# A two-layer cross-attention kernel: the context of later batches loaded in 32x32 blocks and turned by VectorE, and a new order for the work that prepares the next batch

## The chip, the cores and the metric

The kernel runs on one core of a Trainium2 chip. The metric is the device time of one execution in microseconds; lower is better. Three runs are given as their median, and one further execution was recorded by the profiler.

## The reference

Four sequences of 1024 rows, `x` of width 512 and a context of width 384, go through two cross-attention layers in float32. Cut to what matters:

```python
def layer0(x, context):                      # 16 heads of 64
    h = layernorm(x) * gamma + beta
    Q, K, V = h @ Wq, context @ Wk, context @ Wv
    attn = softmax(Q @ K.T, axis=-1) * 64 ** -0.5          # per head
    return x + (attn @ V) @ Wo + bo

def layer1(x, context):                      # 16 heads of 32
    xn = x * rsqrt(mean(x * x) + 1e-5) * norm_w
    q, k, v = xn @ wq, *split(context @ wkv)
    q, k = l2_normalised(rotary(q)), l2_normalised(rotary(k))
    attn = softmax(q @ k.T * sqrt(32), axis=-1)
    return x + (attn @ v) @ wout

out = layer1(layer0(x, ctx), ctx)            # the same context in both
```

## The kernel before

The batches are worked one after another. For each of them layer 0 goes through eight pairs of heads, each in eight steps of 128 query rows; then layer 1 goes through two halves of eight heads, each in 32 steps. TensorE multiplies with the feature dimension on the partitions, so it needs both the context and the normalised `x` turned: `cT` (tag `ctxT`, one buffer, 128 x 3 x 1024) and `hT` (two halves of 128 x 4 x 512).

The order in which instructions are issued is written out by the kernel itself; the scheduler does not move them. Every engine works through its own queue in that order. A class `Units` holds a queue of small pieces of other work, each with an estimated cost. Each attention step calls `fill(us)`, which issues pieces until the allowance of the step is spent. A piece with cost 0.0 is issued as soon as its turn comes. In layer 1 the allowance is the total cost left divided by the steps left, so the pieces are spread evenly.

A step of layer 1 (`Attention1.step`) issues, in this order: eight score matmuls (L576) for 128 keys times two and 256 queries; two exponentials on ScalarE (L586) into one of two halves of the tile `e`; the product of the step before (`finish`, `product`: L615), which after every fourth step is followed by the row sums, eight matmuls with `ones` (L626) over the tile `both`; then the pieces of other work; and last the additions on VectorE that collect the exponentials (two of L592 a step, and L596 in the two middle steps of four). A reciprocal and a product (L633, L634) divide after every fourth step. The row sums of one group of four are thus issued in the first step of the next group, and need the additions of all four steps.

The second half of layer 1 is where the next batch is prepared (`prepare_units`, `order`). Its pieces are:

- the context: four row tiles `c` of 128 x 384 a half, loaded on SP (L181), turned by TensorE against an identity into PSUM (L190) and copied to `cT` by ScalarE (L136);
- `x`: four tiles `xr` of 128 x 512 a half (L272), statistics on VectorE (L214, L215), a reciprocal square root on GpSimd (L168), the application on VectorE (L231), a turn on TensorE (L246) and a scaled copy on ScalarE (L248);
- the projections of the first two pairs of heads of the next batch: keys `k` and values `v` from `cT`, queries `q` from `hT` (helper `matmul`, L164);
- the additions of this batch's own first two output groups to `x` (`adds`, split in six parts by `some(i)`): two projection pieces for each of eight row tiles, and one VectorE addition (L294).

The tiles `c` and `xr` share the tag `row` with four buffers, so each group of four must be turned before the next can be loaded. The weights of a pair (tag `wpair`, two buffers) are loaded by `begin` of the pair before (L306). All of these loads are issued by SP, in order, and a load whose buffer is not free stops SP until it is.

The cost of preparing is paid in three of the four batches, since the first is prepared before anything else and has its own order.

Of the kernel before, what the change touches and what calls it, by code (L numbers as in the profile page):

```python
# [31 lines left out]
F32 = mybir.dt.float32  # L32
# [4 lines left out]
P = 128  # L37
S = 1024
NT = S // P
DQ = 512  # L40
NQ = DQ // P
DC = 384
NC_ = DC // P
# [65 lines left out]
def xattn_kernel(ctx: ExitStack, tc: tile.TileContext, a: dict, out: bass.AP):  # L109
    nc = tc.nc  # L110
    x, c = a["x"], a["ctx_768"]
# [3 lines left out]
    sb = ctx.enter_context(tc.tile_pool(name="sb", bufs=2))  # L115
# [10 lines left out]
    def bank(name):  # L126

        while True:
            which["n"] = which["n"] + 1 if which["n"] < 3 else which["from"]
            if which["n"] != which["kept"]:  # L130
                break
            which["kept"] = None
        return ps_f.tile([P, 512], F32, tag=f"f{which['n']}", name=name)

    def evac(dst, src):
        nc.scalar.copy(dst, src)  # L136
# [22 lines left out]
    def matmul(o, lhsT, rhs, start, stop):  # L159

        w = P // which["cols"]
        for j in range(which["cols"]):
            rr = slice(j * w, (j + 1) * w)
            nc.tensor.matmul(o[rr], lhsT[:, rr], rhs, start=start, stop=stop)  # L164
# [5 lines left out]

    def context_units(b, ct):

        raws = {}

        def load(h):
            for t in range(4 * h, 4 * h + 4):
                if b == 0 and h:
                    raws[t] = sb.tile([P, S], F32, tag="vals", bufs=4, name=f"c_{b}_{t}")[:, :DC]
                else:
                    raws[t] = sb.tile([P, DC], F32, tag="row", bufs=4, name=f"c_{b}_{t}")  # L180
                nc.sync.dma_start(raws[t], c[b, t * P : (t + 1) * P, :])  # L181

        def turn_over(h, k):
            if k == 0:
                if h == 0:
                    both = sb.tile([P, NC_, S], F32, tag="ctxT", bufs=1, name=f"cT_{b}")
                    ct.extend([both[:, :, :512], both[:, :, 512:]])
            pp = bank(f"ptc_{b}_{h}_{k}")
            for t in range(4):
                nc.tensor.transpose(pp[:, t * P : (t + 1) * P], raws[4 * h + t][:, k * P : (k + 1) * P], ident)  # L190
            evac(ct[h][:, k, :], pp)

        return [
            {
                "load": [(0.0, lambda h=h: load(h))],
                "turn": [(0.45, lambda h=h, k=k: turn_over(h, k)) for k in range(NC_)],
            }
            for h in range(2)
        ]
# [109 lines left out]
    def pair_units(b, p, w, hT, ct, res):  # L309

        n = f"{b}_{p}"

        def project(what, src, w0, nk, h, k, st={}):
            if what == "kT" and h == 0 and k == 0:
                qk = sb.tile([P, 2, S], F32, tag="qk", bufs=3, name=f"qk0_{n}")
                res["kT"], res["qT"] = qk[:, 0], qk[:, 1]
            if k == 0:
                st["pp"] = bank(f"p{what}0_{n}_{h}")
            matmul(st["pp"], w()[:, w0 + k, :], src[h][:, k, :], k == 0, k == nk - 1)
            if k < nk - 1:  # L320
                return
            if what == "qT":
                evac(res[what][:, h * 512 : (h + 1) * 512], st["pp"])
            else:
                quarters = res[what].rearrange("p (g c i) -> p c g i", g=4, i=32)
                evac(quarters[:, 4 * h : 4 * h + 4], st["pp"].rearrange("p (c g i) -> p c g i", g=4, i=32))

        def values(h, t, st={}):
            if h == 0 and t == 0:
                res["v"] = sb.tile([P, NT, P], F32, tag="v", bufs=3, name=f"v0_{n}")  # L330
            if t == 0:
                st["pp"] = bank(f"pv0_{n}_{h}")
            for k in range(NC_):
                matmul(
                    st["pp"][:, t * P : (t + 1) * P],
                    ct[h][:, k, t * P : (t + 1) * P],
                    w()[:, NQ + NC_ + k, :],
                    k == 0,
                    k == NC_ - 1,
                )  # L340
            if t == 3:
                evac(res["v"][:, 4 * h : 4 * h + 4, :].rearrange("p t f -> p (t f)"), st["pp"])

        return {
            "k": [(0.86, lambda h=h, k=k: project("kT", ct, NQ, NC_, h, k)) for h in range(2) for k in range(NC_)],
            "q": [(0.86, lambda h=h, k=k: project("qT", hT, 0, NQ, h, k)) for h in range(2) for k in range(NQ)],
            "v": [(0.66, lambda h=h, t=t: values(h, t)) for h in range(2) for t in range(4)],
        }
# [296 lines left out]
    def flat(lists):  # L645
        return [u for lst in lists for u in lst]

    def prepare_units(b):

        st = {"ct": [], "hT": [], "pairs": [{} for _ in range(NPAIR)]}  # L650
        w = {}

        def load():
            w[0] = pair_load(b, 0)

        def project(p):
            def begin():
                if p + 1 < NPAIR:
                    w[p + 1] = pair_load(b, p + 1)

            begin = {"begin": [(0.0, begin)]}
            return begin | pair_units(b, p, lambda: w[p], st["hT"], st["ct"], st["pairs"][p])

        st["project"] = lambda p: flat(project(p).values())
        cts = context_units(b, st["ct"])
        norms = norm_units(b, 0, st["hT"], load_rows(b))

        def order(other):

            pairs = [project(p) for p in range(2)]  # L670
            n = len(other)

            def some(i):
                return flat(other[n * i // 6 : n * (i + 1) // 6])

            if b == 0:
                loads = [cts[0]["load"], cts[1]["load"], norms[0]["load"], [(0.0, columns_load)]]
                loads += [norms[1]["load"], pairs[0]["begin"], [(0.0, constants_load)]]
                first = cts[0]["turn"] + norms[0]["stats"] + pairs[0]["k"][:NC_] + norms[0]["apply"]
                first += cts[1]["turn"] + pairs[0]["k"][NC_:] + norms[1]["stats"]  # L680
                first += norms[0]["turn"] + pairs[0]["q"][:NQ] + norms[1]["apply"]
                rest = pairs[0]["v"] + norms[1]["turn"] + pairs[0]["q"][NQ:]
                later = flat([pairs[1][c] for c in ("begin", "k", "q", "v")])
                return [(0.0, load)] + flat(loads) + first, rest, later
            return flat(
                [
                    [(0.0, load)] + cts[0]["load"] + some(0) + cts[0]["turn"],
                    cts[1]["load"] + some(1) + cts[1]["turn"],
                    norms[0]["load"] + some(2) + norms[0]["stats"] + pairs[0]["begin"] + pairs[0]["k"],
                    norms[0]["apply"] + some(3) + norms[0]["turn"],  # L690
                    norms[1]["load"] + pairs[0]["v"] + norms[1]["stats"] + some(4),
                    norms[1]["apply"] + some(5) + norms[1]["turn"] + pairs[0]["q"],
                    pairs[1]["begin"] + pairs[1]["k"] + pairs[1]["q"],
                ]
            ), pairs[1]["v"]

        return st, order

# [2 lines left out]
    first, rest, later = order([])  # L701
# [13 lines left out]
    for b in range(B):  # L715
        ct, hT, pairs = st["ct"], st["hT"], st["pairs"]
# [6 lines left out]
        for p in range(NPAIR):  # L723
# [10 lines left out]
            elif p % 2 == 0:  # L734
                i = p // 2 - 1
# [3 lines left out]
                    lambda n, i=i: wo[i][:, n % 2, :],  # L739
# [6 lines left out]
            if p == 6:  # L746
# [5 lines left out]
                k = rotated_chains(lambda kq=kq: kq["k"], ct, NC_, lambda k, wk=wk: wk[:, k, :], f"k1_{b}_0", RowScratch())  # L752
                other = [(0.0, lambda: begin("k"))] + k[0][0] + flat(outs[:2]) + k[1][0] + k[0][2] + flat(outs[2:4])
            if p == NPAIR - 1:
# [5 lines left out]
                norms = norm_units(b, 1, xnT, lambda h: xt[4 * h : 4 * h + 4])  # L760
                v = []
# [10 lines left out]
            n = 7 * (p == 0)  # L772
# [10 lines left out]
            for i in range(NT):  # L783
# [8 lines left out]
                n = NT * (NPAIR - p) - i  # L792
# [16 lines left out]
        kT, qT = kq["k"], kq["q"]  # L809
        kT1, qT1 = qk_tile(f"k1_{b}_1"), sb.tile([P, 2, S], F32, tag="raw", bufs=1, name=f"q1_{b}_1")  # L810
        q = rotated_chains(lambda kq=kq: kq["q"], xnT, NQ, lambda k, wq=wq: wq[0][:, k, :], f"q1_{b}_0", tmp)
# [19 lines left out]
        for half in range(2):  # L831
            n = 0
            if half == 0:
                vs = value_chains(att1.v1, wv1, ct, f"pv1_{b}_1")
                first = [q[1], (norms[1]["stats"], [], []), vs[0], (norms[1]["apply"], [], k1[1][2]), k1[2]]
# [11 lines left out]
            else:  # L847
# [4 lines left out]
                if b + 1 < B:  # L852
                    st, order = prepare_units(b + 1)
                    first, later = order(adds)
# [24 lines left out]
            kT, qT, v = kT1, qT1, att1.v1  # L879
# [48 lines left out]
```

## Time and profile before

| | |
|---|---|
| median of three runs | 2922.01 us (2919.55 to 2923.83) |
| the profiled execution | 2913.88 us, span 2912.1 us |
| granted TensorE clock, mean | 0.999 |
| TensorE busy | 2852.3 us (98%) |
| VectorE busy | 2186.5 us (75%) |
| ScalarE busy | 1434.4 us (49%) |
| GpSimd busy | 935.1 us (32%) |
| turns of the context on TensorE (L190) | 96 of 128x128, 24 for each batch |
| copies of turned context on ScalarE | 24 of 128x512, mean 608 ns |
| turns of the attention weights on VectorE (L400) | 512 of 128x1024, mean 1229 ns |
| context loads | 32 of 192 KB, 3.8 us to landing (median) |

The busy shares are of the whole span. A busy TensorE is not TensorE at its peak, because matmuls overlap and their ends are modelled. A timeline row gives the start, the time from the first start to the last end of the merged instructions, the engine, and in brackets the idle time before it and what ended it. A row of the stretches gives, for each engine in turn (TensorE, its weight loads, VectorE, ScalarE, GpSimd), its busy time and number of instructions, then the granted clock, the mean busy share of the 16 DMA engines and the rate in GB/s. A row of waits gives the total, the number and the longest.

### The profile page before, as it was taken

The page shows a single profiled execution, that of the slowest core. Times are in us where ns is not written, and L with a number is a line of the kernel's source. Part 1 is how long each engine was busy: PE and PEld are TensorE (multiplying, and loading weights), DVE is VectorE, ACT ScalarE, POOL GpSimd, SP SyncE. Part 2 cuts the span into 40 slices and gives each one's busy share as a digit, 9 for nine tenths or more (in the row PEclk, how much of TensorE's full clock was granted, in tenths as well). Part 3 has the DMA queues.
Part 4 walks back from the last instruction along what each step waited for, and adds up shares of the span by engine and source line. Part 5 has one row for each costly group of instructions (what it writes and reads, how often), then busy time and mean ns, then how long its engine had stood idle before and what let it go on. Part 6 is the DMA issues. An engine that isn't in the chain of part 4 may idle for free.

```text
span 2912.1 us, 66608 instructions
## 1 busy us (share of the span) xinstructions
PE 2852.3 (98%) x27336; PEld 1433.1 (49%) x27336; DVE 2186.5 (75%) x2952; ACT 1434.4 (49%) x2265; POOL 935.1 (32%) x776
## 2 busy tenths in 40 slices
PE   8999999999999999999999999999999999999998
PEld 4444455555444444555544445455554445445544
DVE  5677785878777778587777777858777777785877
ACT  4444444666534444466644444446664444444664
POOL 2343353420134335432024433534102343353300
PEclk9999999999999999999999999999999999999999
DMA  5887775010398777401039887730104988772000
GB/s 142 191 185 184 167 171 127 22 36 25 79 198 191 181 173 174 117 22 36 26 88 213 193 184 166 177 91 22 36 25 113 210 192 187 163 174 74 2 2 31
DMA packets 177553, 348.88 MB, mean 120 GB/s; under 512 B 37600, under 2 KB 93152, under 8 KB 177248
## 3 DMA queue, kind: packets, MB, share of 16 engines
q1 hardware_dynamic: 175920, 343.96, 50.1%
q8 instruction: 216, 3.54, 0.5%
q14 instruction: 89, 0.73, 0.1%
q10 hardware_dynamic: 1328, 0.66, 0.1%
HBM read 67.64 MB, written 8.39 MB: 26 GB/s over the span
## 4 chain that ended last, share of the span: by engine, by line
PE 84%; DVE 8%; SPq 3%; DMA 2%; issue 1%; ACT 1%; POOL 1%; DVEq 0%; ACTq 0%
PE s L366 16%; PE av L427 14%; PE po L164 11%; PE s L576 8%; PE pv L164 7%; PE pqT L164 7%; PE av L615 7%; PE pkT L164 5%; PE q_p L164 3%; SPq L411 2%; PE av L626 2%; PE k_p L164 2%; DVE both L592 2%; DMA eT<-e 1%; DVE both L596 1%
## 5 line engine op out<-in xcount | busy, mean ns | idle before, releaser
L391 DVE TENSOR_REDUCE m<-s 128x1 f32<-128x1024 f32 x512 | 603.0, 1219 | 374.9 <-PE s L366 374.4
L586 ACT ACTIVATE e<-s 128x1024 f32<-128x1024 f32 x512 | 496.7, 1022 | 312.4 <-PE s L576 303.9
L397 POOL TENSOR_SCALAR raw<-raw,li 128x1024 f32<-128x1024 f32 x256 | 286.1, 1118 | 724.2 <-DVE li L396 715.7
L366 PE MATMUL s<-qk 64*128 64x512 f32 x2048 | 515.5, 615 | 2.9 <-ACT e L392 2.2
L392 ACT ACTIVATE e<-s,m 128x1024 f32<-128x1024 f32 x256 | 282.9, 1110 | 466.5 <-DVE m L391 217.4
L392 ACT ACTIVATE raw<-s,m 128x1024 f32<-128x1024 f32 x256 | 285.3, 1115 | 454.8 <-DVE m L391 454.8
L427 PE MATMUL av<-eT,v 128*64 128x256 f32 x4096 | 470.1, 382 | 8.2 <-DMA eT<-e 6.9
L397 POOL TENSOR_SCALAR e<-e,li 128x1024 f32<-128x1024 f32 x256 | 286.0, 1118 | 474.3 <-DVE li L396 247.7
L592 DVE TENSOR_TENSOR both<-e 128x512 f32<-128x512 f32 x512 | 341.9, 700 | 114.2 <-ACT e L586 86.9
L427 PEld LDWEIGHTS av<-eT,v 128*64 128x64 f32 x4096 | 286.2, 137 | 227.2 <-issue 88.6
L366 PEld LDWEIGHTS s<-qk 64*128 64x128 f32 x2048 | 183.7, 186 | 281.5 <-issue 165.4
L576 PE MATMUL s<-q,k 32*128 32x256 f32 x4096 | 306.0, 401 | 5.8 <-ACT q L503 2.7
L400 DVE STREAM_TRANSPOSE e<-raw 128x1024 f32<-128x1024 f32 x256 | 309.9, 1228 | 0.4 <-DMA eT<-e 0.4
L400 DVE STREAM_TRANSPOSE e<-e 128x1024 f32<-128x1024 f32 x256 | 310.0, 1229 | 0.2
L576 PEld LDWEIGHTS s<-q,k 32*128 32x128 f32 x4096 | 192.1, 184 | 152.7 <-ACT e L586 71.4
L164 PE MATMUL pqT<-hT,w 128*64 128x512 f32 (+1 forms) x1216 | 240.6, 595 | 2.4 <-ACT hT L248 2.4
L164 PE MATMUL po<-wo,vals 128*64 128x512 f32 x1024 | 234.6, 596 | 0.0
L294 DVE TENSOR_TENSOR x<-x,po 128x512 f32<-128x512 f32 x200 | 131.2, 678 | 89.4 <-PE po L164 88.8
L164 PEld LDWEIGHTS pv<-w,cT 128*64 128x64 f32 (+1 forms) x3360 | 170.4, 132 | 41.6 <-issue 34.8
L164 PE MATMUL pv<-w,cT 128*64 128x128 f32 (+1 forms) x3360 | 184.3, 274 | 0.7 <-ACT hT L248 0.7
L164 PE MATMUL pkT<-cT,w 128*64 128x512 f32 (+1 forms) x912 | 183.7, 598 | 0.0
L596 DVE TENSOR_TENSOR both<-both 128x1024 f32<-128x1024 f32 x128 | 159.7, 1248 | 4.4
(81 smaller groups left out, 2784.6 us busy)
## 6 DMA issues: line engine op xcount, KB each, us to landing
eT<-e SPq DMA_DIRECT2D x2048, 128.0 KB, 2.4
xr<-in_x_dram SPq DMA_DIRECT2D x32, 256.0 KB, 3.8
wo<-in_Wo_dram SPq DMA_DIRECT2D x16, 512.0 KB, 4.7
x<-in_x_dram SPq DMA_DIRECT2D x32, 256.0 KB, 3.8
out_dram<-x SPq DMA_DIRECT2D x32, 256.0 KB, 2.6
w<-in_Wq_dram SPq DMA_DIRECT2D x31, 256.0 KB, 3.1
c<-in_ctx_dram SPq DMA_DIRECT2D x32, 192.0 KB, 3.8
wkv<-in_wkv_dram SPq DMA_DIRECT2D x16, 384.0 KB, 3.3
```

The costliest lines, as they stand in the source:

```text
L164: nc.tensor.matmul(o[rr], lhsT[:, rr], rhs, start=start, stop=stop)
L366: nc.tensor.matmul(sc[j][:, kb * 512 : (kb + 1) * 512], pr["qT"][r[j], i * P : (i + 1) * P], pr["kT"][r[j], kb * 512 : (kb + 1) * 512], st ...
L391: nc.vector.tensor_reduce(m[:, j : j + 1], sc[j], AX.X, ALU.max, negate=True)
L392: nc.scalar.activation(e[j], sc[j].rearrange("p (g s) -> p g s", g=4), AF.Exp, bias=m[:, j : j + 1], accum_out=l[:, j : j + 1])
L397: nc.gpsimd.tensor_scalar(e[j], e[j], li[:, j : j + 1], HD0**-0.5, ALU.mult, ALU.mult)
L400: self.turn = [lambda j=j: nc.vector.transpose(self.e[:, :, i % BQ * 2 + j, :], e[j]) for j in range(2)]
L427: nc.tensor.matmul(av[r[j], :W].rearrange("p (t a i) -> p t a i", t=BQ, a=4), pr["v"][:, k, r[j]], eT[:, j, :, :, k * 32 : (k + 1) * 32], ...
L576: nc.tensor.matmul(sc[j // 2][:, j % 2, c, :], kT[rr, g, k * P : (k + 1) * P], qT[rr, g, qb * WQ : (qb + 1) * WQ], start=True, stop=True,)
L586: nc.scalar.activation(e, sc[u], AF.Exp, scale=float(np.sqrt(np.float32(HD1))))
L592: nc.vector.tensor_add(self.both[:, kk, 2 * u : 2 * u + 2, :], es[u][:, :, 0, :], es[u][:, :, 1, :])
L596: nc.vector.tensor_add(self.both[:, 0], self.both[:, 0], self.both[:, kk])
L615: nc.tensor.matmul(self.av[rr, 0, :], v[g][:, 2 * kk + c, rr], es[j // 2][:, j % 2, c, :], start=first and c == 0, stop=end and c == 1,)
```

## The change

For the later three batches the context is no longer loaded as rows. Twelve DMAs write it straight into `cT`, each taking 32 features of all 1024 rows to 32 partitions, in pieces of 32 floats, so that every 32x32 block stands at its place but is not turned. Six VectorE instructions then turn the blocks in place, each over 128 x 512. The turns on TensorE and the copies on ScalarE are gone for these batches. The first batch keeps the old way.

The order of the pieces in the second half of layer 1 is also new. `x` is loaded, normalised and turned first, then the queries of both pairs are projected; the turn of the context's blocks comes after that, and the keys and values of pair 0 and the keys of pair 1 stand at the end. A small condition in `project` lets the queries of a pair come before its keys.

```diff
     def context_units(b, ct):
         raws = {}
+        def load_blocks():
+            both = sb.tile([P, NC_, S], F32, tag="ctxT", bufs=1, name=f"cT_{b}")
+            ct.extend([both[:, :, :512], both[:, :, 512:]])
+            rows = c[b].rearrange("(n i) m -> i n m", i=32)
+            for k in range(NC_):
+                for g in range(4):
+                    f = k * P + g * 32
+                    dst = both[g * 32 : (g + 1) * 32, k, :].rearrange("p (n m) -> p n m", m=32)
+                    nc.sync.dma_start(dst, rows[:, :, f : f + 32])
+
+        def turn_blocks(k):
+            for h in range(2):
+                nc.vector.transpose(ct[h][:, k, :], ct[h][:, k, :])
+
+        if b > 0:
+            return {
+                "load": [(0.0, load_blocks)],
+                "turn": [(0.0, lambda k=k: turn_blocks(k)) for k in range(NC_)],
+            }
...
         def project(what, src, w0, nk, h, k, st={}):
-            if what == "kT" and h == 0 and k == 0:
+            if not "kT" in res:
                 qk = sb.tile([P, 2, S], F32, tag="qk", bufs=3, name=f"qk0_{n}")
...
-            return flat(
+            first = flat(
                 [
-                    [(0.0, load)] + cts[0]["load"] + some(0) + cts[0]["turn"],
-                    cts[1]["load"] + some(1) + cts[1]["turn"],
-                    norms[0]["load"] + some(2) + norms[0]["stats"] + pairs[0]["begin"] + pairs[0]["k"],
-                    norms[0]["apply"] + some(3) + norms[0]["turn"],
-                    norms[1]["load"] + pairs[0]["v"] + norms[1]["stats"] + some(4),
-                    norms[1]["apply"] + some(5) + norms[1]["turn"] + pairs[0]["q"],
-                    pairs[1]["begin"] + pairs[1]["k"] + pairs[1]["q"],
+                    [(0.0, load)] + norms[0]["load"] + cts["load"] + some(0) + norms[0]["stats"] + some(1),
+                    norms[0]["apply"] + some(2) + norms[0]["turn"],
+                    norms[1]["load"] + some(3) + norms[1]["stats"] + pairs[0]["begin"] + pairs[0]["q"][:NQ] + some(4),
+                    norms[1]["apply"] + some(5) + norms[1]["turn"] + pairs[0]["q"][NQ:],
+                    pairs[1]["q"] + cts["turn"] + pairs[0]["k"] + pairs[0]["v"] + pairs[1]["begin"] + pairs[1]["k"],
                 ]
-            ), pairs[1]["v"]
+            )
+            return first, pairs[1]["v"]
```

## The prediction

> **What bounds the kernel now.** First the page's busy shares, then a table of stretches: the second halves of layer 1, in which the next batch is prepared, run from about 628 to 755 us, 1351 to 1478 and 2069 to 2196; the change lies in these three alone.
>
> ```profile
> PE 2852.3 (98%) x27336; PEld 1433.1 (49%) x27336; DVE 2186.5 (75%) x2952; ACT 1434.4 (49%) x2265; POOL 935.1 (32%) x776
> ...
> 632.00:745.00 113.00, 112.73 (x1596) 58.35 (x1592) 86.47 (x121) 72.74 (x87) 3.07 (x4) 1.00 0.13 39
> ```
>
> TensorE is busy 112.7 of 113 us there. Work taken off it is time gained, unless a wait replaces it; and any wait of TensorE is lost for good. VectorE is busy 86.5 of 113, so it has slack on the mean, not in every step. The list of waits shows where its slack ends:
>
> ```profile
> PE av L626 <- DVE both L592: 15.4, 9, 2.2
> ```
>
> Line 626, the row sums, comes every fourth step and needs VectorE's additions (L592, L596) of the step before; 15.4 us in nine places is TensorE's largest wait of its own. The timeline of TensorE prices what is removed:
>
> ```profile
> 634.37 1.53 PE L190 MATMUL ptc<-ident,c 128*128 128x128 f32 x12
> 635.94 1.07 PE L164 MATMUL po<-wo,o 128*32 128x512 f32 x8
> ...
> 642.17 1.53 PE L190 MATMUL ptc<-ident,c 128*128 128x128 f32 x12
> 643.63 1.15 PE L576 MATMUL s<-q,k 32*128 32x256 f32 x16
> ```
>
> Twelve transposes take 635.94 - 634.37 = 1.57 us, and the second twelve 643.63 - 642.17 = 1.46. The timeline of VectorE gives the prices that the change shuffles (from one start to the next):
>
> ```profile
> 632.43 0.69 DVE L294 TENSOR_TENSOR x<-x,po 128x512 f32<-128x512 f32 x1 [4.47 <-PE po L164]
> 633.03 1.29 DVE L592 TENSOR_TENSOR both<-e 128x512 f32<-128x512 f32 x2
> 634.24 1.75 DVE L633 RECIPROCAL rest<-rest 128x256 f32<-128x256 f32 x1
> 636.02 0.42 DVE L634 TENSOR_TENSOR o<-rest 128x256 f32<-128x256 f32 x1
> 636.36 1.29 DVE L592 TENSOR_TENSOR both<-e 128x512 f32<-128x512 f32 x2
> ...
> 655.42 0.69 DVE L214 BATCH_NORM_STATS2 st<-xr 128x6 f32<-128x512 f32 x1
> ...
> 658.62 1.26 DVE L592 TENSOR_TENSOR both<-e 128x512 f32<-128x512 f32 x2
> 659.92 1.22 DVE L596 TENSOR_TENSOR both<-both 128x1024 f32<-128x1024 f32 x1
> 661.06 2.57 DVE L592 TENSOR_TENSOR both<-e 128x512 f32<-128x512 f32 x4
> ...
> 665.82 1.91 DVE L231 TENSOR_SCALAR xr<-xr,mv,rs 128x512 f32<-128x512 f32 x4
> 667.65 1.28 DVE L592 TENSOR_TENSOR both<-e 128x512 f32<-128x512 f32 x2
> ```
>
> An x addition is 0.60, a pair of L592 1.21 (1.31 ahead of L596), L596 1.14, reciprocal and product 1.78 + 0.34, four statistics 3.20, four applications 1.83. Before the change, statistics come in step 6 and their application two steps later, after line 626 has passed.
>
> **What the Trainium skill says.** "VectorE: DVE Perf Modes", The three transpose paths: VectorE turns 32x32 blocks only, which is why the load must place the blocks; the trace has such an instruction (L400, 1229 ns for 128x1024). "TensorE: Matmul & The Clock Gate", Part 4: a TensorE transpose lands in PSUM and needs a copy after it; the trace agrees (24 copies cT<-ptc, 609 ns at the median), and its 273 ns per record overlaps, so I use 0.13. "DMA: Bandwidth & Descriptors", Specifications: below 512 B a transfer misses the full rate, by a read-modify-write; no 128 B load is in this trace. The same page, Queues, rings and completion order: each engine takes descriptors in ring order, so what SP issues after the blocks moves after them.
>
> **The change, part by part** (three times each).
>
> Removed: 24 TensorE transposes a batch, 1.57 + 1.46 = 3.03 us, all on the path: -3.0. Their six ScalarE copies (0.61 each) lay beside other work: 0, since ScalarE is busy 73 of 113 us; one 0.15 us wait for such a copy goes too.
>
> Added, VectorE: six turns of 128x512, in place. Half of 1229 ns is 0.61; with the fixed part I take 0.65, 3.9 us a batch. They stand in step 21, behind the reciprocal and product. In the corresponding step of before the product starts at 727.72, and TensorE comes to its projections at 728.68. The first turn is done near 728.8, so the first key projection waits about 0.15; later ones need a turn every 1.3 us and find it. The pairs of additions behind the turns come 3 us late; counted on, the last is ready near 738.1 where line 626 asks at 739.4: no wait. If that cover of 1.3 us were gone, up to 2.6 us a batch.
>
> Added, SP: twelve DMAs in place of eight, 128 KB each in 1024 pieces of 128 B. They wait for the last value projection of the half before (near 627), since the turned tile has one buffer; SP stands still meanwhile, as it did for c_4. Behind them on SP: the second four rows of x, then the weights of pairs 1, 2 and 3. Price per piece and engine: the three weight loads at 722 us, 1280 pieces of 512 B, show
>
> ```profile
> DMA packets 1329, 0.67 MB, mean 84 GB/s; under 512 B 48, under 2 KB 1328, under 8 KB 1328
> ...
> q1 hardware_dynamic: 1328, 0.66, 29.3%
> ```
>
> 0.293 x 8 us x 16 / 1280 = 29 ns. The 16 B pieces of cols, at 11 to 12 us, leave about 8 ns each (15.1 us of engine time less 131 x 95 ns for the x rows, over some 360). I take 8 to 29 ns: 768 pieces an engine, 6 to 22 us, and twelve issues of 0.5 us (the 512-piece load) to 1 us beside them. Done by 637 to 652. The second rows of x wait until 654.5 for their buffers anyway: hidden. Above about 36 ns it is not (rival 2).
>
> Moved: the order. x goes first; its first rows load at 560, with no wait. But now statistics stand in step 1, their application in step 2, with an x addition in each of steps 0, 1 and 2. VectorE starts x_0 at 632.43 (TensorE's first sum, unmoved) and then has, ahead of line 626 in step 4: 0.60 + 1.21 + 1.78 + 0.34 + 3.20 + 0.60 + 1.31 + 1.14 + 1.83 + 0.60 + 1.31 + 1.14 + 1.28 = 16.3 us, with no gap: ready at 648.8. TensorE, at 3.79 us for a step with two units and 2.93 with one, starts steps 1 to 4 at 632.3, 636.1, 639.9 and 642.8, and asks at 645.0. Line 626 and everything behind it wait, and end at 649.2, not 645.8: **+3.4 us**. Next, x_4's sum is ready at 658.4 and VectorE goes on: 0.60 + 1.31 + 1.14 + 3.20 + 1.28 = 7.5, to 666.0; the row sums of step 8 ask for it at 664.9: **+1.2**. In step 12 nothing is late (681.2 against 681.5).
>
> Small change: a step with one unit is so short that the next scores wait 0.22 us for an exponential (729.65, where they take 1.37 in place of 1.15). Before has three such steps, the new order six more or less undisturbed ones: +0.7. A wait of 0.36 at 662 goes.
>
> Sum a batch: -3.03 - 0.15 + 0.15 + 3.4 + 1.2 + 0.7 - 0.36 = +1.9 us. Three batches: +5.7. Against the profiled execution (span 2912.1, time 2913.88) that makes 2919.6. This execution lies 8.1 under the median of the three runs, so I forecast 2922.0 + 5.7 = 2927.7.
>
> The later part of the half: the weights of pair 1 come behind the blocks, near 660, wanted in step 16; those of pair 2 wait for pair 0's values, near 742 instead of 722, and are wanted near 764. Loads take 4.5 us: 0.
>
> **Rivals.**
>
> 1. *Faster: VectorE's crowd is absorbed.* If TensorE's waits in steps 4 and 8 stay under 1 us together, what is left is -3.0 + about 0.5: 7.5 us less in all, to 9 at the most: 2913 to 2914.5. For it: VectorE's mean of 77% in the half. Against: the 16.3 us are uninterrupted and have no room to shrink. 22%.
>
> 2. *Slower: blocks late.* The 128 B pieces cost more than the 512 B ones, by the read-modify-write of the skill. The point: 36 ns, where the queue is free only at 655. At 58 ns (twice 29) the blocks end at 627 + 44.5 + 2.5 = 674, the x rows at 677; the statistics, due at 661.5, stand 15 us and hold every addition behind them: +15 x 3 + 5.7 = +51, 2973. At 45 ns 5 us: +21, 2943. For it: that sentence. Against: the 16 B pieces at 8 ns. 15%.
>
> 3. *The waits of the row sums shorter or longer.* The main case with its steps off by 1.7 us a batch either way: +0.6 to +11, 2922.6 to 2933, which is its own range. 60%, about half of it beyond 0.2%. That the program does not do what the change says is excluded by its order of instructions; 3% is left for no net change by other causes.
>
> **The numbers.** About 0.2% (5.8 us) is what a measurement here tells from no change. Faster: rival 1 but for the part that falls under 5.8, 21%. Same: 30 of the main case, that part and the rest, 34%. Slower: 30 of the main case and rival 2, 45%. The range takes in rival 1 from below and part of rival 2 from above: 2912 to 2942.
>
> **What would show it.** After: no L190 rows past 50 us; TensorE's wait at the row sums for VectorE (15.4 us now) up by 10 to 17; two such waits a batch, near 645 to 649 and 665; VectorE without a gap from 632 to 649. Steps 21 to 24 without a wait over 0.5. The blocks landed before 655 and no wait of the statistics for x. Wrong if the row sums of step 4 do not wait, or if the statistics wait for a DMA.

## The result and the profile after

The changed kernel takes 2932.44 us (median of four, 2929.78 to 2937.41), the kernel before 2920.78 in the same comparison (2917.57 to 2923.83). The ratio is 1.0044, with a 95% interval of 1.0030 to 1.0058: 9 to 17 us slower.

TensorE issues 72 instructions fewer and is busy longer; a slower clock, of which more below, makes the same work last longer. The page of the kernel after, and a row of its stretches that covers the same 113 us of the half as the row shown of before (the half starts 4.5 us later in this execution):

```profile
PE 2862.6 (98%) x27264; PEld 1433.3 (49%) x27264; DVE 2195.0 (75%) x2970; ACT 1426.4 (49%) x2247; POOL 937.3 (32%) x776
```

```profile
636.50:749.50 113.00, 109.79 (x1532) 55.33 (x1528) 87.33 (x125) 68.06 (x79) 3.08 (x4) 0.98 0.12 26
```

TensorE was busy 112.7 of 113 us and now is busy 109.8, with a mean clock of 0.98: it stands idle for 3.2 us of them, where it stood for 0.3. The list of TensorE's waits (total, times, longest) names what for:

```profile
PE av L650 <- DVE both L616: 17.0, 12, 2.2
PE av L650 <- DVE both L620: 7.3, 3, 2.4
```

These are the row sums (L626 of before, now L650), which waited 15.4 us in nine places. Those nine lie outside the three halves that the change touches, so they do not show, as the prediction has it, that VectorE's slack ended there. In each of the three halves TensorE's list has a single row in the kernel before, and it is another wait:

```profile
PE pv L164 <- ACT hT L248: 0.2, 1, 0.2
```

The three further waits in the first row of the kernel after are 0.5 us each, in step 8 of the three halves. The second row is new, and is one wait, in step 4, for each of the three batches. The timelines show it for the first batch. VectorE:

```profile
636.95 0.69 DVE L318 TENSOR_TENSOR x<-x,po 128x512 f32<-128x512 f32 x1 [4.47 <-PE po L164]
...
640.88 0.69 DVE L238 BATCH_NORM_STATS2 st<-xr 128x6 f32<-128x512 f32 x1
...
645.98 1.23 DVE L620 TENSOR_TENSOR both<-both 128x1024 f32<-128x1024 f32 x1
647.13 1.91 DVE L255 TENSOR_SCALAR xr<-xr,mv,rs 128x512 f32<-128x512 f32 x4
...
652.01 1.28 DVE L616 TENSOR_TENSOR both<-e 128x512 f32<-128x512 f32 x2
655.87 0.69 DVE L318 TENSOR_TENSOR x<-x,po 128x512 f32<-128x512 f32 x1 [2.57 <-PE po L164]
```

No row between the first and the second last has a bracket: VectorE works from 636.95 to 653.29 without a gap. TensorE in the same time:

```profile
647.33 1.37 PE L600 MATMUL s<-q,k 32*128 32x256 f32 x16
648.63 1.07 PE L639 MATMUL av<-e,rest 128*32 128x256 f32 x16
652.15 2.27 PE L650 MATMUL av<-both,ones 128*32 128x256 f32 x16 [2.44 <-DVE both L620]
653.85 1.96 PE L164 MATMUL po<-wo,o 128*32 128x512 f32 x8
655.75 0.66 PE L270 MATMUL pth<-ident,xr 128*128 128x128 f32 x4
656.33 1.15 PE L600 MATMUL s<-q,k 32*128 32x256 f32 x16
```

The first and the last row are the score matmuls that begin steps 4 and 5: step 4 takes 656.33 - 647.33 = 9.00 us, where it took 4.66 in the kernel before.

After the wait, two more things are to be seen. The sixteen row sums take 2.27 us, where sixteen that wait for nothing take 1.05 (at 761.23); the second eight of them need the last additions, which end at 653.29. The eight projections behind them wait for nothing and take 1.96, where eight of the same shape take 1.04 elsewhere in this half (at 663.13). In the stretches around the wait, the column behind the five busy times is the granted TensorE clock:

```profile
645.00:650.00 5.00, 4.70 (x68) 2.18 (x60) 4.96 (x9) 1.94 (x2) 0.55 (x1) 1.00 0.02 3
650.00:655.00 5.00, 2.85 (x22) 1.22 (x24) 3.26 (x5) 2.47 (x3) 0.00 (x0) 0.70 0.00 0
655.00:660.00 5.00, 4.94 (x54) 2.85 (x48) 4.10 (x6) 3.32 (x5) 0.00 (x0) 0.96 0.00 0
```

The mean clock is 0.70 in the stretch with the wait. Read in stretches of 1 us, it is 1.00 up to 651, 0.98 in the next, 0.50 in the three from 652 to 655, 0.81 in the next, and 1.00 from 656 on. That is half the clock for about 3.4 us, beginning some 2.3 us after TensorE fell idle. The prediction has no such term.

The blocks are no trouble. The queues in the window from 630 to 650 us, SP's timeline, and the group of the turns:

```profile
q1 hardware_dynamic: 12480, 1.57, 50.5%
```

```profile
631.70 10.00 SPq L187 DMA_DIRECT2D cT<-in_ctx_dram  x12
659.64 0.35 SPq L296 DMA_DIRECT2D xr<-in_x_dram  x1
```

```profile
L191 DVE STREAM_TRANSPOSE cT<-cT x18: 667/669/704, 721.3 to 2174.9; 128x512 f32<-128x512 f32 x18
```

12480 packets in 50.5% of 16 x 20 us are 12.9 ns a packet on each of the 16 engines. The twelve are issued in 10 us and each lands 3.2 us later at the median, so all are there by about 645, fifteen microseconds ahead of the next load on SP. A turn takes 669 ns.

### The profile page after: what moved, and what is told of

It is laid out like the page before. It is cut to its first block, busy times and chain, and to the rows that moved or that the text cites. A ratio compares the mean times of both kernels' runs of the same rounds, so it can differ in the third digit from the quotient of the medians.

```text
span 2933.0 us, 66479 instructions
## 1 busy us (share of the span) xinstructions
PE 2862.6 (98%) x27264; PEld 1433.3 (49%) x27264; DVE 2195.0 (75%) x2970; ACT 1426.4 (49%) x2247; POOL 937.3 (32%) x776
## 4 chain that ended last, share of the span: by engine, by line
PE 82%; DVE 10%; SPq 3%; DMA 2%; ACT 2%; issue 2%; POOL 1%; DVEq 0%; ACTq 0%
PE s L390 16%; PE av L451 14%; PE po L164 10%; PE pv L164 8%; PE s L600 7%; PE pqT L164 7%; PE av L639 6%; PE pkT L164 5%; PE q_p L164 3%; SPq L435 3%; PE av L650 2%; DVE both L616 2%; PE k_p L164 2%; DVE both L620 1%; DVE m L415 1%
## 5 line engine op out<-in xcount | busy, mean ns | idle before, releaser
L620 DVE TENSOR_TENSOR both<-both 128x1024 f32<-128x1024 f32 x128 | 159.7, 1248 | 4.4
```

Of the source, the lines that this page charges most:

```text
L620: nc.vector.tensor_add(self.both[:, 0], self.both[:, 0], self.both[:, kk])
```

## The experiments

One length is read from every trace: **the second half of layer 1**, from its first score matmul to the first score matmul of the next batch. In the first of the three batches, before and then after:

```profile
627.63 1.15 PE L576 MATMUL s<-q,k 32*128 32x256 f32 x16
...
754.59 1.99 PE L366 MATMUL s<-qk 64*128 64x512 f32 x8
```

```profile
632.15 1.15 PE L600 MATMUL s<-q,k 32*128 32x256 f32 x16
...
762.21 1.99 PE L390 MATMUL s<-qk 64*128 64x512 f32 x8
```

The half is 126.95 us in the kernel before and 130.05, 130.03 and 130.02 in the kernel after, +3.08 a batch and +9.2 in all. **Half 0**, the first half of layer 1, whose code is unchanged, is read in the same way, to the first score matmul of the second half: it takes 130.45 us in all batches of before, and 132.12, 130.44, 132.13 and 131.91 in the kernel after. Within a half, the length of a step runs from its first score matmul to that of the next.

| kernel | second half, three batches | half 0, four batches | time against before, 95% |
|---|---|---|---|
| before | 126.95 126.96 126.95 | 130.45 130.44 130.45 130.45 | |
| after | 130.05 130.03 130.02 | 132.12 130.44 132.13 131.91 | 1.0030 to 1.0058 |
| e1_order | 130.33 130.32 130.32 | 130.45 130.44 132.08 130.45 | 1.0022 to 1.0042 |
| e2_stats0 | 125.89 125.88 125.89 | 132.07 132.05 131.94 132.08 | 0.9998 to 1.0015 |
| e3_no_turn | 129.06 130.01 129.97 | 130.44 130.45 130.44 130.45 | 1.0029 to 1.0055 |
| e4_filler | 129.06 129.06 129.05 | 132.08 130.45 130.45 130.44 | 1.0017 to 1.0042 |
| e5_both_stats | 124.77 124.77 124.77 | 132.05 130.42 132.09 132.05 | 0.9985 to 1.0008 |
| e6_both_stats_filler | 124.77 124.77 124.78 | 130.40 130.41 130.41 130.41 | 0.9952 to 0.9979 |
| e7_before_filler | 126.94 126.94 126.95 | 130.41 130.41 130.41 130.42 | 0.9977 to 0.9993 |
| e8_one_filler | 129.06 129.05 129.04 | 132.06 132.07 130.42 130.42 | 1.0025 to 1.0044 |
| e9_blocks | 131.02 131.98 132.43 | 132.05 130.42 130.42 130.42 | 1.0027 to 1.0054 |
| e10_blocks_spread | 130.03 130.23 129.88 | 132.05 130.42 132.05 130.43 | 1.0030 to 1.0055 |
| e11_blocks_spread_filler | 130.98 129.86 130.25 | 130.43 130.43 130.41 130.43 | 1.0027 to 1.0052 |
| e12_early_x | 132.32 133.29 132.52 | 130.45 130.45 130.45 130.45 | 1.0034 to 1.0059 |

The theory, called A in most of the expectations, is that the work costs that VectorE has in its queue ahead of the row sums. The rivals are that the blocks themselves cost (their turns or transfers), or that the order costs in another way.

**The order alone** (e1_order). The context of later batches stays as rows and is turned by TensorE, between the queries.

```diff
-                    [(0.0, load)] + norms[0]["load"] + cts["load"] + some(0) + norms[0]["stats"] + some(1),
+                    [(0.0, load)] + norms[0]["load"] + some(0) + norms[0]["stats"] + some(1),
...
-                    pairs[1]["q"] + cts["turn"] + pairs[0]["k"] + ...
+                    pairs[1]["q"][:NQ] + cts[0]["turn"] + cts[1]["load"] + pairs[1]["q"][NQ:] + cts[1]["turn"] + pairs[0]["k"] + ...
```

> The new order alone: x first, keys and values last, but the context still comes as rows and is turned by TensorE (24 transposes and 6 ScalarE copies for each later batch), and VectorE turns nothing. The second half of layer 1 took 126.95 us before and 130.03 to 130.05 after, in each of three batches. Theory A (the order costs, by VectorE's crowd in steps 0 to 4, and the turn on VectorE is nearly free): the transposes come back, 3.0 us, the VectorE turn goes, 0.15: 132.9 us a half, and +18 us in all against before. Theory B (what costs is the turn on VectorE or the loading in blocks, and the order is harmless): about 127 us a half, and no difference from before.

Measured were 130.3 us a half, 3.37 more than before, with no block in the kernel. The order costs by itself. A had expected 132.9, which is 2.6 too much. The timeline of TensorE in e1_order (its lines are five lower) says why the blocks, added to this order, gave back only 0.3 of the 3.03 us of transposes:

```profile
644.90 1.07 PE L634 MATMUL av<-e,rest 128*32 128x256 f32 x16
647.78 0.64 PE L645 MATMUL av<-both,ones 128*32 128x256 f32 x8 [1.81 <-DVE both L615]
648.98 1.23 PE L645 MATMUL av<-both,ones 128*32 128x256 f32 x8 [0.56 <-DVE both L611]
```

The wait is there, but in two pieces (1.81 and 0.56), and the granted clock is 1.00 in all stretches of 5 us from 645 to 660. With the work spread otherwise, step 4 takes 7.34 us here and 9.00 in the kernel after, step 8 4.49 and 5.98. The saved transposes brought TensorE sooner to the same waits, and 0.97 us of the difference in step 4 is the clock's, as shown below.

**The first statistics out of the way** (e2_stats0).

```diff
-                    [(0.0, load)] + norms[0]["load"] + cts["load"] + some(0) + norms[0]["stats"] + some(1),
+                    [(0.0, load)] + norms[0]["load"] + cts["load"] + norms[0]["stats"] + some(0) + some(1),
```

> After, with one piece moved: the statistics of the first four x tiles stand in step 0, ahead of the first x addition, where VectorE idles 4.5 us for TensorE's sum. Theory A: the chain ahead of the row sums in step 4 is 3.2 us shorter, the wait there falls from 3.6 us or so to about 0.5, and TensorE's clock no longer falls behind it: 126 us a half in place of 130.05, -12 us in all against after and -2 to -3 against before. Theory B (the order is harmless): no difference from after.

Measured were 125.9 us, as A said, and the row of L620 is gone from TensorE's list of waits. Step 4 falls from 9.00 to 4.84 us. One move in VectorE's queue of four statistics is worth 4.15 us a batch and turns the half's +3.08 into -1.07. The time is no less than before's, though (0.9998 to 1.0015), where A had 2 to 3 us less: all four half 0s took 132 us in the profiled execution, which is looked into below.

**No turn** (e3_no_turn). The six turns are left out, so later batches compute keys and values from unturned blocks.

```diff
-                    pairs[1]["q"] + cts["turn"] + pairs[0]["k"] + pairs[0]["v"] + ...
+                    pairs[1]["q"] + pairs[0]["k"] + pairs[0]["v"] + ...
```

> After without the six VectorE turns (the context of the later batches stays in unturned blocks, so keys and values come from wrongly ordered data). Theory A (the turn stands in a step with slack): a half is 0.15 us shorter, 129.9, and the whole within 1 us of after. Theory B (VectorE's time is on the path): 3.6 to 4 us shorter a half, 126.2, -12 us in all.

Measured were 130.0 us in two batches, as with the turns. So the turns are hidden. In the remaining batch, the first, the half took 129.06: there TensorE waits the same 2.44 us in step 4, but the clock is at 1.00 in every stretch of 1 us from 642 to 656. From 648.23 to 650.06 the sixteen row sums take 1.83 us, 0.78 more than without a wait, so they do stand for the last additions. With the 2.44 ahead that is a wait of 3.2 us.

**Work put into the wait**, matmuls whose result is not used, called filler (e4_filler, then e8_one_filler with one matmul in place of three).

```diff
             if end:
+                if half == 1 and g == 0 and qb == 0 and self.b < B - 1:
+                    idle = bank(f"idle_{n}")
+                    for _ in range(3):
+                        nc.tensor.matmul(idle, ident, bo, start=True, stop=True)
                 for i in (0, NT // 2 - 1):
```

> After with work added: three 128x512 matmuls of the identity on a constant tile, 2.6 us of TensorE, ahead of the row sums of step 4, where TensorE waits for VectorE; their result is not used. Theory C (the idle wait makes TensorE's clock fall to half for some us, which adds 1.1 us a batch to a wait of 3.4): the wait is filled, the clock stays at 1.0 in the stretch behind it, and a half takes 129.0 us, 1.1 less, though TensorE does more. Rival (the clock is not the cause): the added work is hidden in the wait at best, 130.05, or costs up to 2.6 us a half.

> The changed kernel with one 128x512 identity matmul (its result is overwritten) ahead of the row sums of step 4, in place of the three tried before: about a third of the 2.4 us that TensorE waits is filled. If a shorter idle stretch is enough to keep the clock, the second half lasts 129.06 as with three; if the fall depends on the stretch being wholly broken up, 130.0 in some or all batches.

Measured were 129.06 us with either, in all batches. TensorE has more to do and is done 0.97 us sooner. A stretch around the wait in e4_filler (clock 1.00, TensorE busy throughout), and the timeline of TensorE in e8_one_filler:

```profile
653.00:658.00 5.00, 5.00 (x33) 1.89 (x32) 3.38 (x6) 2.53 (x3) 0.00 (x0) 1.00 0.00 0
```

```profile
650.51 1.13 PE L650 MATMUL idle<-bo,ident 128*128 128x512 f32 x2
653.02 1.61 PE L654 MATMUL av<-both,ones 128*32 128x256 f32 x14 [1.38 <-DVE both L620]
```

With one filler TensorE still waits 1.38 us, and the clock holds at 1.00 in the stretch from 651 to 656. So the 0.97 us are the clock's, and come from TensorE's standing idle. The Trainium skill has the mechanism ("TensorE: Matmul & The Clock Gate", Part 1: The HAM clock gate): the clock is halved after an idle window of about 3.4 us and given back after about as long of sustained work, in a window that runs on by itself, so that where the change falls varies from run to run. The 3.4 us at half clock agree with the page, and so does the variation: the wait of 2.44 us brought the fall in five batches of six and not in the first of e3_no_turn. That a wait of 2.44 us is enough does not agree with an idle window of 3.4 us; for the length that it takes the measurement decides.

**Both statistics moved** (e5_both_stats): the move of e2_stats0, and

```diff
-                    norms[1]["load"] + some(3) + norms[1]["stats"] + pairs[0]["begin"] + pairs[0]["q"][:NQ] + some(4),
+                    norms[1]["load"] + pairs[0]["begin"] + pairs[0]["q"][:NQ] + norms[1]["stats"] + some(3) + some(4),
```

> The change with both of layer 1's second-half statistics moved: the first to the head of step 0 (ahead of the q turns), the second behind the q evictions of step 2. Step 4's row sums then follow a VectorE that has only evictions and exponentials' sums ahead (4.84 us for step 4 was measured with the first move alone), and step 8, 5.98 us with the first move alone, should come down to about 4.7. Theory A (the VectorE chain ahead of the row sums is what costs): the second half of layer 1 lasts about 124.5 us per later batch, 2.4 less than in the kernel before and 5.5 less than in the changed kernel; about 7 us faster than the kernel before if half 0 keeps its clock in as many batches. Theory B (step 8's length comes from elsewhere, or the moved statistics only make step 12 wait): 125.9 as with the first move alone.

Measured were 124.77 us. Step 8 falls from 5.98 to 4.66 (4.7 expected), and step 12 takes 0.22 longer. In TensorE's list of waits the row sums are back at what they had before the change:

```profile
PE av L650 <- DVE both L616: 15.4, 9, 2.2
```

The half is now 2.18 us shorter than before the change. The time is not shorter: 0.9985 to 1.0008, where 7 us less were expected. Three of the four half 0s took 132 us.

**Work put into half 0's wait**, on that version (e6_both_stats_filler) and on the kernel before (e7_before_filler).

```diff
             if end:
+                if half == 0 and g == 0 and qb == 3:
+                    for _ in range(5):
+                        nc.tensor.matmul(self.av[:, 1, :], ident, bo[:, :WQ], start=True, stop=True)
                 for i in (0, NT // 2 - 1):
```

> The kernel with both statistics moved, and five 128x256 matmuls with the identity (their result is overwritten) ahead of the row sums of step 28 in half 0 of layer 1, where TensorE waits 2.2 us for VectorE. If the granted clock falls because TensorE idles there, half 0 lasts 130.4 to 130.5 us in all four batches and the clock stays at 1.00 after step 28; second halves as without the filler (124.5). Against the kernel before: about 7 us faster, and up to 10 if half 0 falls in most executions of the kernel before. If the fall has another cause, half 0 still takes 132.1 in some batches, or 130.5 plus up to 1 us for the added matmuls.

> The kernel before with only the five 128x256 identity matmuls ahead of the row sums of step 28 in half 0. If half 0's two lengths (130.45 and 132.1) are the clock's fall in the 2.2 us wait, all four half 0s last 130.45 and the time falls by 1.65 us times the mean number of batches in which the kernel before loses its clock: 0 to 4 us, about 2. If the lengths have another cause, the time is the same or up to 2 us longer, and 132.1 still occurs. The second half of layer 1 stays 126.95.

Step 28 of half 0 has a wait of 2.2 us for VectorE in the kernel before as well. In the kernel after, the clock falls behind it, again to half for about 3.4 us (read in stretches of 1 us). The timeline of TensorE, and a stretch:

```profile
617.16 1.22 PE L650 MATMUL av<-both,ones 128*32 128x256 f32 x6 [2.23 <-DVE both L616]
...
618.19 3.18 PE L164 MATMUL pv<-wkv,cT 128*32 128x256 f32 x22
```

```profile
618.00:621.00 3.00, 3.00 (x28) 1.21 (x20) 2.47 (x3) 0.59 (x1) 2.92 (x2) 0.50 0.00 0
```

The same place in e7_before_filler, with the added matmuls first:

```profile
615.88 2.42 PE L625 MATMUL av<-bo,ident 128*128 128x256 f32 x10
618.24 1.37 PE L629 MATMUL av<-both,ones 128*32 128x256 f32 x14
...
619.45 1.67 PE L164 MATMUL pv<-wkv,cT 128*32 128x256 f32 x22
```

The same 22 projections take 3.18 us at clock 0.50 and 1.67 here. In the four versions with this filler all sixteen half 0s last 130.4; in the ten profiles without it 17 of 40 last about 132. The profile of the kernel before shows none of those, so the test on that kernel is its time: it gains 0.0007 to 0.0023 (2.0 to 6.7 us) from work that computes nothing. At 1.65 us a fall that makes one to four falls an execution. That the kernel before has such executions fits its other runs: of the 52 beside this experiment, the five with a mean clock of 0.999 took 2915.4 us on average and the six with 0.995 took 2925.9. On the changed kernel with both statistics moved the filler gives the best version: 2913.27 us at the median, ratio 0.9966 (0.9952 to 0.9979), 6 to 14 us faster than the kernel before.

**The blocks alone** (e9_blocks): the order of before, with the six turns behind the first statistics.

```diff
-                    [(0.0, load)] + cts[0]["load"] + some(0) + cts[0]["turn"],
-                    cts[1]["load"] + some(1) + cts[1]["turn"],
-                    norms[0]["load"] + some(2) + norms[0]["stats"] + pairs[0]["begin"] + pairs[0]["k"],
+                    [(0.0, load)] + cts["load"] + some(0) + some(1),
+                    norms[0]["load"] + some(2) + norms[0]["stats"] + cts["turn"] + pairs[0]["begin"] + pairs[0]["k"],
```

> The other part alone: later batches' context in blocks turned by VectorE, with the second half of layer 1 in the order of the kernel before (keys and values of the pair first, then x). Six turns of 0.67 us stand directly behind the four statistics (3.4 us), 7.4 us of VectorE work in a row where the kernel before had 3.4. Theory A (what decides is what VectorE has to do ahead of each batch of row sums): TensorE saves 3.03 us per batch, but the row sums of step 8 are ready some 35.3 us after the half's start and asked for at 30.9 to 31.5, so they wait about 4 us: the second half lasts 127 to 128.5, no shorter than the 126.95 of the kernel before. Theory B (the order alone costs, and the blocks are worth their transposes): 123.9 to 124.5.

Measured were 131.0 to 132.4 us, worse than either theory. TensorE does wait for what stands late in VectorE's queue, but not where A had put it. In this order the keys come right after the turns, and it is they that wait; from the list of TensorE's waits:

```profile
PE pkT L164 <- DVE cT L191: 14.2, 3, 4.7
```

Step 4 takes 10.68 us (4.66 before), of it 4.7 of waiting; the clock is at 0.82 and 0.84 in the two stretches of 5 us from 655 on. Step 8, where A had put the wait, takes 4.66.

**The blocks alone, VectorE's pieces apart** (e10_blocks_spread), the same with half 0's filler (e11_blocks_spread_filler), and with the second load of x earlier (e12_early_x).

```diff
-                    norms[0]["load"] + some(2) + norms[0]["stats"] + cts["turn"] + pairs[0]["begin"] + pairs[0]["k"],
-                    norms[0]["apply"] + some(3) + norms[0]["turn"],
-                    norms[1]["load"] + pairs[0]["v"] + norms[1]["stats"] + some(4),
+                    norms[0]["load"] + some(2) + cts["turn"] + some(3) + pairs[0]["begin"] + pairs[0]["k"] + norms[0]["stats"],
+                    pairs[0]["v"][:NC_] + norms[0]["apply"] + pairs[0]["v"][NC_:] + norms[0]["turn"],
+                    norms[1]["load"] + norms[1]["stats"] + some(4),
```

> As the blocks alone, with VectorE's two pieces kept apart: the turns stay where they are (behind step 3's row of exponentials), the statistics of the first half of x move behind the keys, after the row sums of step 8, and the short steps between are filled from the output projections. Theory A: step 8 waits 1 to 1.5 us instead of 4 (the kernel before waits about 0.4 there), so the second half lasts 124.5 to 125.2; the time falls by 5 to 7 us against the kernel before, if half 0 and layer 0 lie as there. Theory B, that the place of VectorE's work does not matter: the same as the blocks alone.

> The spread version with the five 128x256 identity matmuls (their result is overwritten) ahead of the row sums of step 28 in half 0. Half 0 lasts 130.41 in all four batches; second halves as in the spread version. Against the kernel before: 5 to 7 us from the second halves and about 4.4 us from half 0, as measured for the filler alone: 9 to 12 us faster (ratio 0.996 to 0.997), as fast as the version with both statistics moved and the filler.

Measured were 129.9 to 131.0 us in the two versions, not 124.5 to 125.2. The part that was aimed at came out: step 4 takes 4.88, step 8 5.16, and the first sixteen steps 61.36 us against 63.60 in the kernel before. Then step 16 takes 10.97. The edit had left nothing between the second load of x and its statistics; from the timelines of VectorE and TensorE in e10_blocks_spread:

```profile
688.28 0.69 DVE L238 BATCH_NORM_STATS2 st<-xr 128x6 f32<-128x512 f32 x1 [3.46 <-DMA xr<-in_x_dram]
```

```profile
694.73 0.64 PE L650 MATMUL av<-both,ones 128*32 128x256 f32 x8 [1.66 <-DVE both L620]
697.16 1.25 PE L650 MATMUL av<-both,ones 128*32 128x256 f32 x6 [1.79 <-DVE both L616]
```

VectorE stood 3.46 us for the rows, and the additions behind the statistics carried that to the row sums. The clock falls here too, to 0.77 in the stretch from 695 to 700, though neither of the two waits reaches 1.8 us and 0.64 us of row sums lie between them. In e1_order 1.81 and 0.56 us, broken in the same way, left it at 1.00. So a break of that kind does not always keep the clock; how much of the idle time has to be filled was not measured further. Half 0 held 130.4 with the filler (e11), as expected; the time, 9 to 12 us under before, did not come.

```diff
-                    norms[1]["load"] + norms[1]["stats"] + some(4),
-                    norms[1]["apply"] + some(5) + norms[1]["turn"] + pairs[0]["q"],
+                    norms[1]["load"] + some(4) + some(5)[:3] + norms[1]["stats"],
+                    some(5)[3:] + norms[1]["apply"] + norms[1]["turn"] + pairs[0]["q"],
```

> The spread version with the filler, and the second half of x loaded one stretch of output projections before its statistics instead of directly ahead of them; the statistics stand behind the row sums of step 16. In the spread version step 16 took 10.97 us because VectorE stood 3.46 us for those rows of x and the row sums behind it (3.45 us in two waits, then the clock at 0.77). Theory A (VectorE in order ahead of the row sums): step 16 falls to about 4.9, the second half lasts 124.0 to 124.6 us, some 2.5 less than in the kernel before, that is the 3.03 us of transposes less small waits; with half 0 at 130.4 the time falls by 9 to 12 us (ratio 0.996 to 0.997). Theory B (the blocks' turns or their transfers cost TensorE something of their own, whatever the order): not under 126.

Measured: step 16 takes 4.88 us, as expected, but step 17 takes 10.28. The half is 132.3 to 133.3 us, the ratio 1.0047. What had stood between the statistics and the turn of the normalised rows was now ahead of the statistics, and TensorE's turns wait instead; from its list of waits:

```profile
PE pth L270 <- DVE xr L255: 16.5, 3, 5.5
```

So the three versions of the blocks alone wait in three places, each time for something that stands late in VectorE's queue. What the blocks are worth in a good place in the old order was not reached; the first sixteen steps of e10 (2.2 us shorter) are the nearest to it.

## Why the prediction was right, and where its sizes were off

The forecast was 2927.7, "about +5.7", with slower the likeliest single outcome at 45%. Measured were 11.7 us between the medians, twice the forecast. The direction and the mechanism were right. That 2932.4 lies in the range is less of a merit: 2912 to 2942 would have held a faster kernel too, and the forecast change was no larger than the 5.8 us that the prediction itself takes as its limit.

- **The chain of VectorE.** Forecast were 16.3 us without a gap, from x_0's addition to the last addition that the row sums need. Measured were 16.3, from 636.95 to 653.29. The forecast's 648.8 is 653.3 here less the later start of 4.5.
- **The wait in step 4, +3.4.** The versions, taken one after another, divide the half's +3.08. Without the fall of the clock (e4) the half is 0.97 shorter; without the statistics ahead (e2 against e4) it is another 3.18 shorter; without the second ones (e5 against e2) another 1.11; what is left is 124.77, 2.18 under before. So the wait was right, at 3.18. **The step that was mis-sized** is this term: it stops at the wait, and the TensorE that comes out of it runs slow, for 0.97 us more. 3.4 should have been 4.15.
- **The wait in step 8, +1.2.** The half shows 1.11; step 8 itself shows 1.32.
- **What remains**, -2.69 by the prediction's own terms, is -2.18. The late first turn, 0.15, shows as 0.02 to 0.05 in the half (e3 against after). The other half microsecond lies in the short steps or in the transposes' own price; no run tells these two apart.
- **Sum.** -2.18 + 3.18 + 1.11 + 0.97 = +3.08 a batch, not +1.9, and +9.2 in the three. That is inside the interval of 9 to 17 us. The profiled executions differ by 20.9, since they also differ by 4.8 us in half 0 (three falls of the clock against none) and by 6.8 in layer 0, where the code is unchanged.
- **Row sums' waits, forecast up by 10 to 17 us.** They are up from 15.4 to 24.3, by 8.9, a little less. The list counts the idle time ahead of the first row sum (2.44 in step 4), not the stand of 0.78 inside the row.
- **The blocks.** Forecast were 8 to 29 ns a packet and done by 637 to 652. Measured were 12.9 ns, and done by about 645 with the half 4.5 us late. Rival 2, the late blocks, is dead: no statistics waited for x. Since SP's next load came 15 us after the blocks had landed, no run shows what the ring order that the prediction cites would have done to it. Rival 1, that VectorE's crowd is absorbed, fell too. With the statistics elsewhere (e5) both waits are gone, but even then the time came out as before, not 7.5 us less.
- **Steps 21 to 24** had no wait over 0.5, as forecast.

**Layer 0.** A later batch's layer 0 took between 460.7 and 467.6 us over all runs, and nearly all of the spread comes from two steps of its second pair of heads. In these 84 steps (two in each of three batches, 14 profiles) TensorE stands between 0 and 2.9 us for a DMA. In 17 of them the clock falls as well, which adds about 1.7 us: in the second later batch of the kernel after one such step takes 11.2 us in place of 7.2, with 2.2 of waiting and a mean clock of 0.85. All 17 are among the 25 steps that stand for 1.97 us or more; none of the 59 others, which stand for up to 1.94 us, has a fall.

Open: of the twelve changed versions, nine come out 1 to 6 us above what their halves and the filler account for, with the new order (e5: halves -6.5, measured -0.9) and with the old one (e11: +5.9 above); the other three, e1, e9 and e12, lie between 2.6 below and 0.9 above. The intervals reach 3 to 4 us to either side, so part of this may be chance. Layer 0 may hold some of it. The three later batches together took 1389.0 and 1389.1 us there in the two profiles with the old order and no blocks, and 1389.1 to 1400.0 in the twelve others. These are single profiles, so this is a pointer and not shown.

## What to carry to other kernels

Where engines work in order, ask for every wait what stands ahead of the awaited instruction in the other engine's queue, and by when it is due; a mean of 77% busy says nothing of it. Work taken from the busiest engine pays only as far as its partners are ready sooner: here 3.03 us of transposes saved gave 0.3 until four statistics were moved. When a TensorE wait of about 2 us or more can't be removed, add the slow stretch behind it to its price, or fill a good part of it with matmuls that compute nothing. Here the change was faster than the kernel before only with both statistics moved and half 0's wait filled.

## What the runs showed of the hardware

A single wait of 2.0 to 2.9 us lowers TensorE's granted clock to half for about 3.4 us, often but not always. In step 4 this happened behind a wait of 2.44 us in five batches of six, in half 0 behind 2.2 us in 17 of 40, and in layer 0 behind 1.97 us or more in 17 steps of 25. Behind the shorter waits there, up to 1.94 us, it happened in none of 59. Two waits of 1.66 and 1.79 us with 0.64 us of work between them had the same effect (e10). The price was 0.97 us in step 4, where part of the slow time is hidden in the stand for the last additions, 1.65 in step 28 of half 0, and about 1.7 in layer 0. One 128x512 matmul in the wait (1.13 us in two records, 1.38 of idle left) kept the clock in all three batches. This also explains why a half with unchanged code has two lengths, 130.45 and 132.1, from one batch to the next.

Loads in pieces of 128 B went at 12.9 ns a packet on each of 16 engines, 1.57 MB in about 13 us. That is under half the 29 ns that the prediction reads for the 512 B pieces of the weights, but for a quarter of the bytes: 9.9 bytes a ns on each engine against 17.7. So the small pieces do miss the rate of the larger ones, as the Trainium skill says of pieces under 512 B ("DMA: Bandwidth & Descriptors", Specifications); whether by a read-modify-write, no run shows.
